# Turning an expert tile's token rows and another tile's gated values together, in 64-row halves of the TensorE array

## The chip, the cores and the metric

The kernel runs on one core of a Trainium2 chip. The metric is the device time of one execution in microseconds (us), taken as the median of several runs. Beside it stands one execution that was profiled; times of single instructions come from that one.

## What is computed

Two transformer layers on x of shape 8 x 512 x 256, all in fp32. The first is an attention with relative positions and a feed-forward block with a token-dependent low-rank part; the second a masked attention and a mixture of experts. Only the last part is changed. Cut to it:

```python
tokens = hidden_states.reshape(-1, 256)              # 4096 tokens
topk_idx, topk_w = route(tokens)                     # 4 of 32 experts for each token
gate_vals = silu(einsum('th,eih->tei', tokens, gate_w))   # gate_w: 32 x 128 x 256
up_vals = einsum('th,eih->tei', tokens, up_w)             # up_w:   32 x 128 x 256
expert_out = einsum('tei,ehi->teh', gate_vals * up_vals, down_w)  # down_w: 32 x 256 x 128
mixed = (take(expert_out, topk_idx) * topk_w[:, :, None]).sum(1)
return mixed + shared_expert(tokens)
```

## The kernel before

Earlier stages leave, for every token and each of its four experts, one row of 264 numbers in a DRAM table `rows`, sorted by expert: 256 values of the token, then the place of its result and its weight. The table is cut into NS = 160 tiles of 128 rows, padded so that a tile belongs to one expert. All experts' weights lie in SBUF as `store`, 768 columns an expert: 256 columns of gate and up for each half k of the 256 inputs (NK = 2), and 256 columns of down.

The last stage goes through the 160 tiles, one per step s of a loop whose order is written by hand (`tc.manual_schedule()`), as a software pipeline over tiles. Names and lines are those of the profile:

- `fetch` (L1414) loads a tile r of 128 x 264, by a DMA on SP's queue, eight tiles ahead (TILES = 8). Eleven buffers (TILES + 3) hold r until its rows are scattered.
- `spread` (L1432, L1434) turns the two 128 x 128 halves of r by two TensorE transposes into a PSUM bank `ptr` and copies 128 x 256 to SBUF as `rT` on DVE. In step s it does tile s + 3.
- `numbers` (L1420) reads eight experts' numbers into TensorE registers, every eighth step, ahead of `expert_hidden`.
- `expert_hidden` (L1440, L1444, L1446) multiplies rT with gate and up into `pge`; each of the two products, 256 columns wide, is two matmul instructions in fp32, so a tile has four. ACT makes silu of the gate half, `acte`, and DVE multiplies by the up half, giving `hide`. In step s it does tile s + 2.
- `turned_hidden` (L1451, L1453) turns hide (one 128 x 128 transpose, PSUM bank `pth`) and copies it to `hidT` on DVE. In step s it does tile s + 1.
- `result` (L1458, L1460, L879) multiplies hidT with down into `poe` (two matmul instructions), ACT scales by the row's weight into y, and POOL issues an indirect DMA that scatters y to the table `results`. In step s it does tile s.
- `gather`, `add`, `put` (L1470, L1482, L1485, L1492): as soon as all tiles that a batch of tokens needs are out, its results are gathered on SP's queue, added on DVE and stored; these pieces are spread over later steps.

So TensorE's order in a step is: two transposes of r for tile s + 3, four product instructions for tile s + 2, one transpose of hide for tile s + 1, two product instructions for tile s. Each of the four PSUM pools (`ps_r`, `ps_t`, `ps_e`, `ps_y`) has two banks[...].

The first attention, elsewhere in the same program, turns its weights e in 64-row halves (`turned`, L412, copied at L415). It matters as the place where such instructions are already in the trace:

```python
for f, bank in enumerate(banks):
    rs, c = slice(64 * f, 64 * f + 64), (j * NT + m) * 64
    nc.tensor.transpose(bank[:, c : c + 64], e[rs, m * P : (m + 1) * P], ident[rs, rs])
```

Around it on TensorE stand transposes of 128 rows ahead (L384), then products of 128 rows by 32 columns of the array (L424), and at times products of the whole array after these (L273).

Of the kernel before, what the change touches and what calls it, by code (L numbers as in the profile page):

```python
# [12 lines left out]
F32 = mybir.dt.float32  # L13
# [5 lines left out]
PSUM = bass.MemoryType.PSUM  # L19
DRAM = bass.MemoryType.DRAM  # L20

P = 128
B, S, H = 8, 512, 256
NT = S // P
NK = H // P
# [16 lines left out]
NS = NTOK * TOPK // P + NE  # L42
TILES = 8
ROW = 264
# [757 lines left out]
def _l1(nc, tc, a, x, out, ident, mhalf, rows, results, filled, inputs, early):  # L802
# [14 lines left out]
    with ExitStack() as ctx:  # L817
        pool = lambda name, bufs, **kw: ctx.enter_context(tc.tile_pool(name=name, bufs=bufs, **kw))
# [14 lines left out]
        for half in range(2):  # L833
            s = slice(half * P, (half + 1) * P)
# [36 lines left out]
        def after(ins, others):  # L871
            info = mybir.DependencyInfo(mybir.DependencyClass.Sync, mybir.DependencyReason.DATA)
            for o in others:
                tc.add_manual_dep(ins.ins, o.ins.name, info, reason="rows of DRAM")
# [32 lines left out]
        q, k, v, xlT = {}, {}, {}, {}  # L907
        prods, sums, sc, softs, values, turned = {}, {}, {}, {}, {}, {}
# [472 lines left out]
        for u in range(U):  # L1381
            t = start[u]
# [21 lines left out]
            experts()  # L1404
        routing.close()
        tp = pool("m_t", 2)
        ps_r = pool("m_psr", 2, space=PSUM)
        ps_t = pool("m_pst", 2, space=PSUM)
        ps_e = pool("m_pse", 2, space=PSUM)
        ps_y = pool("m_psy", 2, space=PSUM)  # L1410

        def fetch(s):
            r = tp.tile([P, ROW], F32, tag="r", name="r", bufs=TILES + 3)
            ins = nc.sync.dma_start(r, rows[s * P : (s + 1) * P, :])  # L1414
            after(ins, scattered["rows"][-16:])
            return r

        def numbers(s):

            _, found = nc.values_load_multi_w_load_instructions(  # L1420
                number[0:1, s : s + 8],
                [mybir.EngineType.PE],
                min_val=0,
                max_val=NE - 1,
                skip_runtime_bounds_check_because="all but the bits of an expert's number are masked out",
            )
            return dict(enumerate(found, s))

        def spread(r):
            pt = ps_r.tile([P, S], F32, tag="psr", name="ptr")  # L1430
            for k in range(NK):
                nc.tensor.transpose(pt[:, k * P : (k + 1) * P], r[:, k * P : (k + 1) * P], ident)  # L1432
            rT = tp.tile([P, H], F32, tag="rT", name="rT", bufs=3)
            nc.vector.tensor_copy(rT, pt[:, :H])  # L1434
            return rT

        def expert_hidden(w, rT):
            pg = ps_e.tile([P, S], F32, tag="pse", name="pge")
            for k in range(NK):
                nc.tensor.matmul(  # L1440
                    pg[:, :H], rT[:, k * P : (k + 1) * P], w[:, k * H : (k + 1) * H], start=k == 0, stop=k == NK - 1
                )
            act = tp.tile([P, P], F32, tag="acte", name="acte", bufs=3)
            nc.scalar.activation(act, pg[:, :P], AF.Silu)  # L1444
            hid = tp.tile([P, P], F32, tag="hide", name="hide", bufs=3)
            nc.vector.tensor_tensor(hid, act, pg[:, P : 2 * P], ALU.mult)  # L1446
            return hid

        def turned_hidden(hid):
            pt = ps_t.tile([P, S], F32, tag="pst", name="pth")  # L1450
            nc.tensor.transpose(pt[:, :P], hid, ident)  # L1451
            hidT = tp.tile([P, P], F32, tag="hidT", name="hidT", bufs=3)
            nc.vector.tensor_copy(hidT, pt[:, :P])  # L1453
            return hidT

        def result(w, r, hid):
            po = ps_y.tile([P, S], F32, tag="psy", name="poe")
            nc.tensor.matmul(po[:, :H], hid, w[:, 2 * H :], start=True, stop=True)  # L1458
            y = tp.tile([P, H], F32, tag="y", name="y", bufs=4)
            nc.scalar.activation(y, po[:, :H], AF.Copy, scale=r[:, H + 1 : H + 2])  # L1460
            scatter("results", results, r[:, H : H + 1].bitcast(U32), y, NTOK * TOPK + NS * P - 1)
# [3 lines left out]
        def gather(u, t, sent):  # L1465

            h, p = divmod(u, 4)
            i = NT * (2 * p + t // 2) + 2 * h + t % 2
            z[u, t] = tp.tile([P, TOPK, H], F32, tag="z", name="z", bufs=5)
            ins = nc.sync.dma_start(  # L1470
                z[u, t].rearrange("p k c -> p (k c)"),
                results[i * P * TOPK : (i + 1) * P * TOPK, :].rearrange("(p k) c -> p (k c)", k=TOPK),
            )
            tc.declare_no_dep(ins.ins, group="results", reason="its results are those sent")
            tc.add_to_no_dep_group("gathers", ins.ins)
            after(ins, sent)

        def add(b, t, part):

            w = z[b, t]  # L1480
            if part == 0:
                nc.vector.tensor_tensor(w[:, :2, :], w[:, :2, :], w[:, 2:, :], ALU.add)  # L1482
            else:
                to = _halves(x, b)[t]
                nc.vector.tensor_tensor(to, to, w[:, part - 1, :], ALU.add)  # L1485

        def put(u, t):

            h, p = divmod(u, 4)
            to = out.rearrange("b (t p) c -> b p t c", p=P)  # L1490
            if isinstance(t, tuple):
                nc.sync.dma_start(to[2 * p + t[0], :, 2 * h : 2 * h + 2, :], two_tiles(u, t[0]))  # L1492
            else:
                nc.sync.dma_start(to[2 * p + t // 2, :, 2 * h + t % 2, :], _halves(x, u)[t])
# [4 lines left out]
        def finish(b, s):  # L1499

            sent = scattered["results"][-16:]
            for t in range(NT):
                beside.setdefault(s + 3 + 3 * t, []).append(partial(gather, b, t, sent))
                for part in range(3):
                    beside.setdefault(s + 8 + 3 * t + part, []).append(partial(add, b, t, part))
            for r in range(2):
                beside.setdefault(s + 22 + r, []).append(partial(put, b, (r,)))

        with tc.manual_schedule():


            tiles, which, rTs, made, hidTs = {}, {}, {}, {}, {}
            weights = lambda s: store[:, bass.ds(which[s], 1), :].rearrange("p e c -> p (e c)")
            for s in range(TILES):
                tiles[s] = fetch(s)
            for s in range(-3, NS):
                if 0 <= s < NS - TILES:
                    tiles[s + TILES] = fetch(s + TILES)
                if s + 3 < NS:
                    rTs[s + 3] = spread(tiles[s + 3])  # L1520
                if 0 <= s + 2 < NS:
                    if (s + 2) % 8 == 0:
                        which.update(numbers(s + 2))
                    made[s + 2] = expert_hidden(weights(s + 2), rTs.pop(s + 2))
                if 0 <= s + 1 < NS:
                    hidTs[s + 1] = turned_hidden(made.pop(s + 1))
                if s < 0:
                    continue
                result(weights(s), tiles.pop(s), hidTs.pop(s))
                for f in beside.pop(s, []):  # L1530
                    f()

                n, more = divmod(s + 2 - NE, S * TOPK // P)
                if 0 < n < B and more == 0:
                    finish(n - 1, s)
            for t in range(NT):
                gather(B - 1, t, scattered["results"][-16:])
            for s in sorted(beside):
                for f in beside[s]:
                    f()  # L1540
            for t in range(NT):
                for part in range(3):
                    add(B - 1, t, part)
                put(B - 1, t)
# [140 lines left out]
```

## Time and profile before

| what | us |
|---|---|
| median of 3 runs | 2083.9 (2081.64 to 2084.47) |
| the profiled execution, whole | 2102.91 |
| its span, first to last instruction | 2101.1 |
| first transpose of the expert tiles starts at | 1816.5 |
| first result product (tile 0) starts at | 1823.9 |
| last result product (tile 159) starts at | 2089.2 |
| TensorE busy in 1834 to 2087 | 249.4 of 253.0 |
| DVE, ACT, POOL busy in the same stretch | 160.6, 112.9, 147.2 |
| granted TensorE clock, 1816 to 1827 and 1827 to 2087 | 0.68 and 1.00 |

In the lines of the profile a matmul instruction's time runs from its start to its modelled end, and instructions overlap in the array; what a stream of them costs is therefore read from one start to the next, not from the sum of times. In a line of the timeline "xN" is a number of instructions on end, the first number where the first of them starts, the second the time from there to the end of the last. "64*128" is the part of the array that an instruction uses, in rows and columns; L1440's and L1458's instructions are "128*128". PEld is the load of the stationary operand, which can run ahead under an earlier matmul.

### The profile page before, as it was taken

The page shows a single profiled execution, that of the slowest core. Times are in us where ns is not written, and L with a number is a line of the kernel's source. Part 1 is how long each engine was busy: PE and PEld are TensorE (multiplying, and loading weights), DVE is VectorE, ACT ScalarE, POOL GpSimd, SP SyncE. Part 2 cuts the span into 40 slices and gives each one's busy share as a digit, 9 for nine tenths or more (in the row PEclk, how much of TensorE's full clock was granted, in tenths as well). Part 3 has the DMA queues.
Part 4 walks back from the last instruction along what each step waited for, and adds up shares of the span by engine and source line. Part 5 has one row for each costly group of instructions (what it writes and reads, how often), then busy time and mean ns, then how long its engine had stood idle before and what let it go on. Part 6 is the DMA issues. An engine that isn't in the chain of part 4 may idle for free.

```text
span 2101.1 us, 49496 instructions
## 1 busy us (share of the span) xinstructions
PE 1930.6 (92%) x17956; PEld 1334.9 (64%) x17956; DVE 1389.0 (66%) x3731; ACT 1106.3 (53%) x2366; POOL 1143.3 (54%) x1340
## 2 busy tenths in 40 slices
PE   7999999999999999999889999879888778599997
PEld 4666667666666666676656666545455455388786
DVE  3677777777777777777676454257876775356666
ACT  2677777767777777677631222345433422144443
POOL 4666777767778686776733111114444443455555
PEclk7999999999999999999989999999989987699999
DMA  8999999999999999899944548601111115457888
GB/s 270 305 317 284 310 303 300 292 289 304 295 297 304 296 306 299 286 289 299 285 140 143 167 141 127 20 1 42 42 42 42 42 42 215 169 163 217 256 254 266
DMA packets 388928, 444.43 MB, mean 212 GB/s; under 512 B 43344, under 2 KB 367952, under 8 KB 388688
## 3 DMA queue, kind: packets, MB, share of 16 engines
q1 hardware_dynamic: 373904, 401.93, 63.9%
q0 software_dynamic: 13824, 38.29, 5.0%
q8 instruction: 145, 2.38, 0.5%
q10 hardware_dynamic: 960, 1.05, 0.1%
q14 instruction: 95, 0.78, 0.1%
HBM read 238.99 MB, written 202.19 MB: 210 GB/s over the span
## 4 chain that ended last, share of the span: by engine, by line
PE 63%; DVE 11%; DMA 11%; issue 5%; POOL 5%; ACT 3%; SPq 1%; another core or an unknown queue 0%; POOLq 0%; DVEq 0%; ACTq 0%
PE sc L372 7%; PE sc L384 6%; PE pge L1440 6%; PE et_ps L412 5%; PE po L684 5%; DMA winp<-shift 5%; PE ctx_ps L424 5%; PE pq L291 5%; PE ph L676 3%; PE poe L1458 3%; PE pa L315 3%; DMA shift<-strip 3%; PE pq L935 2%; PE po L460 2%; DVE prod L796 2%
## 5 line engine op out<-in xcount | busy, mean ns | idle before, releaser
L398 DVE CUSTOM_DVE_ANT_0 e<-sc,winc 128x512 f32<-128x512 f32 x512 | 333.3, 689 | 268.1 <-PE sc L384 139.4
L401 ACT ACTIVATE e<-e,low 128x512 f32<-128x512 f32 x512 | 365.7, 715 | 94.8 <-DVE low L398 93.5
L322 ACT COPY strip<-pa 128x512 f32<-128x512 f32 x512 | 275.2, 591 | 138.6 <-POOL winc L352 58.2
L325 POOL TENSOR_TENSOR own<-aside,strip 128x512 f32<-128x512 f32 x256 | 269.1, 1051 | 130.3 <-ACT strip L322 121.6
L415 DVE COPY et<-et_ps 128x512 f32<-128x512 f32 x512 | 328.5, 683 | 0.7 <-PE et_ps L412 0.7
L372 PE MATMUL sc<-sm,sm 32*128 32x256 f32 (+3 forms) x1792 | 310.5, 437 | 0.2
L315 PE MATMUL pa<-pos,sm 32*128 32x256 f32 x2048 | 297.2, 407 | 1.7 <-ACT sm L299 1.0
L879 POOL DMA_INDIRECT rows<-pay,slot x128 | 141.4, 1105 | 237.2 <-issue 224.9
L352 POOL TENSOR_TENSOR winp<-winp,own 128x256 f32<-128x256 f32 x256 | 187.3, 732 | 108.0 <-DMA winp<-shift 78.3
L372 PEld LDWEIGHTS sc<-sm,sm 32*128 32x128 f32 x1792 | 164.1, 184 | 97.0 <-DVE et L415 35.6
L384 PE MATMUL sc<-ident,winp 128*128 128x128 f32 x1280 | 204.9, 287 | 22.4 <-DMA winp<-shift 21.1
L879 POOL DMA_INDIRECT results<-y,r x160 | 157.0, 981 | 124.3 <-ACT y L1460 70.7
L352 POOL TENSOR_TENSOR winc<-winc,own 128x256 f32<-128x256 f32 x256 | 187.2, 731 | 52.2 <-DMA winc<-shift 40.6
L384 PEld LDWEIGHTS sc<-ident,winp 128*128 128x128 f32 x1280 | 137.4, 142 | 102.0 <-issue 58.3
L315 PEld LDWEIGHTS pa<-pos,sm 32*128 32x128 f32 x2048 | 178.5, 187 | 11.5 <-issue 2.0
L412 PE MATMUL et_ps<-ident,e 64*128 64x64 f32 x4096 | 184.2, 230 | 1.1 <-DVE et L415 1.1
L58 POOL TENSOR_TENSOR rstd<-var,mhalf 128x2 f32<-128x2 f32 (+1 forms) x56 | 51.1, 912 | 241.5 <-DVE var L56 208.9
L412 PEld LDWEIGHTS et_ps<-ident,e 64*128 64x128 f32 x4096 | 148.9, 140 | 44.4 <-issue 22.8
L1440 PE MATMUL pge<-store,rT 128*128 x640 | 168.0, 385 | 3.5 <-DVE rT L1434 1.1
L424 PE MATMUL ctx_ps<-et,v 128*32 128x128 f32 x4096 | 166.6, 281 | 0.5 <-DVE et L415 0.5
L291 PE MATMUL pq<-xnT,wqk 128*128 128x512 f32 x256 | 134.0, 646 | 0.1
L679 ACT ACTIVATE hT<-ph,b 128x512 f32<-128x512 f32 x64 | 44.0, 687 | 165.6 <-PE ph L676 165.5
(216 smaller groups left out, 3339.0 us busy)
## 6 DMA issues: line engine op xcount, KB each, us to landing
shift<-strip SPq DMA_DIRECT2D x256, 510.0 KB
winp<-shift SPq DMA_DIRECT2D x128, 384.0 KB
winc<-shift SPq DMA_DIRECT2D x128, 384.0 KB
winp<-shift SPq DMA_DIRECT2D x128, 256.0 KB
winc<-shift SPq DMA_DIRECT2D x128, 256.0 KB
rows<-empty SPq DMA_DIRECT2D x8, 2640.0 KB
r<-rows SPq DMA_DIRECT2D x160, 132.0 KB
z<-results SPq DMA_DIRECT2D x32, 512.0 KB
```

The costliest lines, as they stand in the source:

```text
L315: nc.tensor.matmul(pa[:, t * W : (t + 1) * W], src[rs, i * P : (i + 1) * P], pos[rs, g, :], start=True, stop=True)
L322: nc.scalar.copy(st[:, 2 * j : 2 * j + 2, :].rearrange("p t w -> p (t w)"), pas[j])
L352: nc.gpsimd.tensor_tensor(dst, dst, own[:, t], ALU.add)
L372: nc.tensor.matmul(sc[:, c0:c1], s[side_][rs, cut : cut + P], s[2 + side_][rs, c0:c1], start=c0 == 0, stop=False, skip_group_check=True,)
L384: nc.tensor.matmul(sc[:, m * P : (m + 1) * P], wins[n + 2 * (m - i)][1][:, j, (i - m + 1) * P : (i - m + 2) * P], ident, start=False, stop ...
L398: nc.vector.tensor_tensor_reduce(e, sc, wins[n][0][:, j, :], 1.0, -LOW, ALU.add, ALU.min, low)
L401: nc.scalar.activation(e, e, AF.Exp, bias=low, scale=-1.0, accum_out=totals[b, g // 2][:, i, r : r + 1])
L412: nc.tensor.transpose(bank[:, c : c + 64], e[rs, m * P : (m + 1) * P], ident[rs, rs])
L415: nc.vector.tensor_copy(et[:, f].rearrange("p j m q -> p (j m q)"), bank)
L424: nc.tensor.matmul(ctx_ps[32 * r : 32 * r + 32, i * P : (i + 1) * P], vs[b % 2][:, m, g % 2, g // 2 * 4 + r, :], et[:, :, m, :], start=m = ...
L879: ins = nc.gpsimd.indirect_dma_start(to, bass.IndirectOffsetOnAxis(ap=index, axis=0), source, None, bounds_check=last)
L1440: nc.tensor.matmul(pg[:, :H], rT[:, k * P : (k + 1) * P], w[:, k * H : (k + 1) * H], start=k == 0, stop=k == NK - 1)
```

## The change

- A new `turned(r, hid)` takes the place of `spread` and `turned_hidden`. In step s it turns r of tile s + 4 and hide of tile s + 1 into one PSUM tile of two banks, each 128 x 128 transpose as two transposes of 64 rows: rows 0 to 63 into the first bank, rows 64 to 127 into the second, the two alternating. One DVE copy moves all 128 x 384 to SBUF.
- `expert_hidden` runs for tile s + 3 in step s, `result` for tile s as before. So hide now lies two steps ahead of where it is turned and not one, and the loop starts at s = -4.
- The PSUM pool `ps_r` goes; `ps_t` holds two tiles of two banks. r has twelve buffers, hide four.
- TensorE's order in a step: six half transposes, four product instructions for tile s + 3, two for tile s. The orders of SP's and POOL's queues stay as they were.

```diff
-            r = tp.tile([P, ROW], F32, tag="r", name="r", bufs=TILES + 3)
+            r = tp.tile([P, ROW], F32, tag="r", name="r", bufs=TILES + 4)
...
-        def spread(r):
-            pt = ps_r.tile([P, S], F32, tag="psr", name="ptr")
-            for k in range(NK):
-                nc.tensor.transpose(pt[:, k * P : (k + 1) * P], r[:, k * P : (k + 1) * P], ident)
-            rT = tp.tile([P, H], F32, tag="rT", name="rT", bufs=3)
-            nc.vector.tensor_copy(rT, pt[:, :H])
-            return rT
+        turns = lambda out, rows: [
+            nc.tensor.transpose(out[:, f, :], rows[64 * f : 64 * f + 64], ident[64 * f : 64 * f + 64, 64 * f : 64 * f + 64])
+            for f in range(2)
+        ]
+
+        def turned(r, hid):
+
+            pt = ps_t.tile([P, 2, S], F32, tag="pst", name="pt")
+            parts = []
+            if r is not None:
+                parts += [(k, r[:, k * P : (k + 1) * P]) for k in range(NK)]
+            if hid is not None:
+                parts.append((NK, hid))
+            for k, rows in parts:
+                turns(pt[:, :, k * 64 : (k + 1) * 64], rows)
+            out = tp.tile([P, NK + 1, 2, 64], F32, tag="turned", name="turned", bufs=3)
+            ks = slice(parts[0][0], parts[-1][0] + 1)
+            nc.vector.tensor_copy(
+                out[:, ks].rearrange("p k f t -> p f k t"),
+                pt[:, :, : (NK + 1) * 64].rearrange("p f (k t) -> p f k t", t=64)[:, :, ks],
+            )
+            return out.rearrange("p k f t -> p (k f t)")
...
-            hid = tp.tile([P, P], F32, tag="hide", name="hide", bufs=3)
+            hid = tp.tile([P, P], F32, tag="hide", name="hide", bufs=4)
...
-        def turned_hidden(hid):
-            pt = ps_t.tile([P, S], F32, tag="pst", name="pth")
-            nc.tensor.transpose(pt[:, :P], hid, ident)
-            hidT = tp.tile([P, P], F32, tag="hidT", name="hidT", bufs=3)
-            nc.vector.tensor_copy(hidT, pt[:, :P])
-            return hidT
...
-            for s in range(-3, NS):
+            for s in range(-4, NS):
...
-                if s + 3 < NS:
-                    rTs[s + 3] = spread(tiles[s + 3])
-                if 0 <= s + 2 < NS:
-                    if (s + 2) % 8 == 0:
-                        which.update(numbers(s + 2))
-                    made[s + 2] = expert_hidden(weights(s + 2), rTs.pop(s + 2))
-                if 0 <= s + 1 < NS:
-                    hidTs[s + 1] = turned_hidden(made.pop(s + 1))
+                if s + 1 < NS:
+                    both = turned(tiles[s + 4] if s + 4 < NS else None, made.pop(s + 1, None))
+                    rTs[s + 4], hidTs[s + 1] = both[:, :H], both[:, H:]
+                if 0 <= s + 3 < NS:
+                    if (s + 3) % 8 == 0:
+                        which.update(numbers(s + 3))
+                    made[s + 3] = expert_hidden(weights(s + 3), rTs.pop(s + 3))
```

More of the change, by code (lines that the diff above doesn't have):

```diff
@@ L1406, in _l1 @@
         tp = pool("m_t", 2)
-        ps_r = pool("m_psr", 2, space=PSUM)
         ps_t = pool("m_pst", 2, space=PSUM)
```

## The prediction, made before the changed kernel had run

> **What bounds the kernel now.** I read the busy times of the page first, then the stretch of the expert tiles alone, then the timeline of TensorE in it. The page says that TensorE is busy for 92% of the span; in the stretch from 1834 to 2087 us it is busy 249.4 of 253.0 us, with the clock at 1.00, while DVE stands at 160.6 and POOL at 147.2. Busy matmul records overlap, so what a tile costs is read from starts:
>
> ```profile
> 1953.61 0.38 PE L1432 MATMUL ptr<-ident,r 128*128 128x128 f32 x2
> 1953.83 1.03 PE L1440 MATMUL pge<-store,rT 128*128 x4
> 1954.70 0.27 PE L1451 MATMUL pth<-ident,hide 128*128 128x128 f32 x1
> 1954.81 0.60 PE L1458 MATMUL poe<-store,hidT 128*128 x2
> 1955.24 0.38 PE L1432 MATMUL ptr<-ident,r 128*128 128x128 f32 x2
> ```
>
> A tile takes 1955.24 - 1953.61 = 1.63 us (1628 ns by the start records), without an idle time in brackets. It is two transposes at 109 ns, four products at 216, one transpose at 109, two products at 217. All are 128*128. So TensorE is the bound here, and whatever changes its instructions moves the end tile by tile. The waits of TensorE in this stretch come to little:
>
> ```profile
> PE pge L1440 <- DVE rT L1434: 1.1, 2, 0.6
> PE poe L1458 <- DVE hidT L1453: 0.9, 1, 0.9
> PE pge L1440 <- ACT y L1460: 0.8, 2, 0.4
> ```
>
> From tile 0's result (1823.88) to tile 159's (2089.24) there are 265.4 us; 159 tiles at 1.628 are 258.8. The 6.6 us left are the only slack that a deeper pipeline can recover. Most of them recur every eighth tile, where the experts' numbers are read into registers (L1420): in the chain of waits, in order of time, such a place reads
>
> ```profile
> 2060.90 0.22 PE ptr L1432 x2
> 2061.12 0.11 issue
> 2061.23 1.10 PE pge L1440 x4
> 2062.33 0.11 PE pth L1451
> ```
>
> 0.3 us late and with four products in 1.10 us, where 1.03 in the timeline above is usual.
>
> **What the changed order will contain.** Half transposes occur already, in the first attention. The timeline of TensorE there:
>
> ```profile
> 803.24 0.87 PE L384 MATMUL sc<-ident,winp 128*128 128x128 f32 x6
> 804.05 0.71 PE L412 MATMUL et_ps<-ident,e 64*128 64x64 f32 x16
> 804.69 0.64 PE L424 MATMUL ctx_ps<-et,v 128*32 128x128 f32 x16
> ...
> 800.53 0.65 PE L424 MATMUL ctx_ps<-et,v 128*32 128x128 f32 x16
> 801.10 1.13 PE L273 MATMUL pv<-wv,xnT 128*128 128x256 f32 x4
> ```
>
> A last start is the end of the group less one instruction's own time: 273 ns for L384 and L424, 223 for L412, 379 for L273 (medians of their lines). Read that way:
> - The last L384 starts at 803.84, the first half at 804.05: 0.20 us (203 ns, the shortest and the median of the 255 such places), where two 128-wide transposes on end stand 109 apart. So 94 ns are lost.
> - Sixteen halves take 0.71 - 0.22 = 0.49 us from first to last start, in pairs: the second pair starts 112 ns after the first, later ones about 63 apart. Six halves: 112 + 63 + 3 = 178 ns.
> - From the last half (804.54) to L424: 150 ns, where 54 to 64 would follow. About 90 are lost again.
> - L273 after L424: 202 ns, not 109, so again 93; and its four products need 1.13 - 0.38 = 0.75 us from first to last start, where L1440 needs 1.03 - 0.38 = 0.65. The first load of weights was not hidden: 104 ns.
>
> [...]
> - [...]every change of the array's form costs 90 to 96 ns beyond the streaming, in both directions.
> - [...]the halves of a pair start 3 to 4 ns apart and a pair takes 63 ns against 109.
> - [...]The first product after a change of form is late by 104[...].
>
> **The change, part by part.**
>
> *Transposes.* Removed: three at 109, 326 ns a tile. Added: six halves between whole-array products, thus two changes of form in every tile. Sum of a tile by the durations above: last product of a tile to the first half 216 + 93 = 309; six halves 178; last half to the first product 150; first to second product 216 + 104 = 320; then the four remaining steps 216, 216, 216, 218 = 866. Together 1823 ns against 1628: 195 ns longer. The three pairs alone, at 63, would have saved 137; the two changes of form with their cold loads cost 332. For 160 tiles: +31.2 us. No instruction stands between 64*128 and 128*128 directly in the trace; I take L424's form for the first and L424 to L273 for the last, as every pair of forms that occurs costs about the same. Bounds: as low as 290 ns for both (the first half's load partly hidden by other work) gives 24.5 us; 350 gives 34.
>
> *Ends of the loop.* Two or three more changes of form in steps without a full set: +0.9 us.
>
> *A step deeper.* hide is made two steps before it is turned. TensorE's queue reaches the read of the numbers earlier, since the load that waited for hide finds it ready; a late read is also covered in part by the cold load that is paid anyway. Of 6.6 us I take 5.5 as gained, a choice, since one place (0.9 us, behind hidT) is of another kind; bounds 0 and 6.6.
>
> *DVE.* Two copies, 418 (128x256) and 283 (128x128), become one. L415's 128x512 takes 682, so a column block of 128 costs about 135 and 128x384 about 550; 150 less a tile. This counts for nothing: DVE is busy 160.6 of 253.0 us. The cover is the 1.8 us of a step; with hide (288) and the largest add (681) DVE needs 1.52 us. If it went over, TensorE would wait by the difference.
>
> *New wait.* The first half transpose waits for r of tile s + 4, hide of tile s + 1 and its two banks, and behind it stand the products of both other tiles, for which ACT, then POOL's scatter wait. hide now comes from products a whole step (1.8 us) further back, and is rarely waited for even today (0.2 us in all by PEld's waits). r is fetched at the same step and used four steps later instead of five: 7.3 us against 8.1; its buffer comes free a tile earlier in exchange (twelve). The tile view has TensorE waiting for r once, at the start, 23.1 us. SP's and POOL's orders stay, and each gets more time per tile. Cost: nothing, bound +5 us if r is late under the gathers.
>
> *Sum.* 31.2 + 0.9 - 5.5 = +26.6 us. The profiled execution of 2102.9 us (span 2101.1) would become 2129.5. The runs' median is 19 us below that execution; this stage is bound by TensorE at full clock, so I carry the difference over: 2083.9 + 26.6 = 2110.5, rounded to 2110.
>
> **Rivals.**
> 1. *Whole gain[...]* (ends faster). If the queue loaded the halves' weights under the products before[...], a tile is 137 ns shorter: -21.9, and -5.5 from the numbers: 2056 us. It decides once both changes cost under 137 + 34 = 171 ns a tile. For it: halves do pair at 63 ns. Against it: the same 203 ns at 255 places, and three other pairs of forms with 93.
> 2. [...]93 + 96 paid, 104 and 49 not. A tile is 43 ns longer: +6.9 + 0.5 - 5.5, so 2086. Against it: 0.75 for L273's four.
> 3. *Worse*: the stalls stay, or r or the copy is late, or the halves run one after another because the banks clash (six at 55 or more, 0.15 us a tile): +38 to +50, 2122 to 2134. Against it: L412's pairs go to two banks in the same way.
> That the order is not as written I exclude: built, TensorE's list shows four halves of r, two of hide, the products, step for step.
>
> **How the numbers follow.** The forecast (2102 to 2119 by its own bounds) has 0.82, the whole gain 0.05, the second rival 0.06, the worse case 0.07. About 0.2% is what a measurement of this kernel can tell from no change, that is 2079.7 to 2088.1: faster 0.05, within 0.05, slower 0.90. The range goes from 2099 (cheap changes and the whole slack) to 2122.
>
> **What would show it.** In the changed trace: a tile period near 1.82 us; about 309 ns from the last result product to the first half; 150 from the last half to a product; four products in about 1.13 us instead of 1.03; one copy of about 550 ns; hardly a gap every eighth tile. A period under 1.63 makes me wrong, and then the gap before the first half, or the first load after the halves, must be shorter than in the first attention. A period above 1.9 with idle TensorE would name r or the copy.

## The result and the profile after

The changed kernel takes 2109.3 us (median of 4 runs, 2106.08 to 2112.87) against 2082.8 (4 runs, 2079.99 to 2084.47): a ratio of 1.0123, 95% interval 1.0100 to 1.0147, or 26.5 us more, where 26.6 were forecast. Its profiled execution, 2110.6 us with a span of 2108.8, lies among its runs. The one of before, 2102.9, lay 19 above its own: there, everything ahead of the expert tiles took 15.6 us longer (first transpose at 1816.5 us, in the changed kernel at 1800.9), which is no part of the change. So spans of these two profiles must not be subtracted; stages can be compared.

The timeline of TensorE in the changed kernel, one tile and the start of the next:

```profile
1954.20 0.34 PE L1430 MATMUL pt<-ident,r 64*128 64x64 f32 x4
1954.38 0.23 PE L1430 MATMUL pt<-ident,hide 64*128 64x64 f32 x2
1954.53 1.13 PE L1455 MATMUL pge<-store,turned 128*128 x4
1955.50 0.59 PE L1466 MATMUL poe<-store,turned 128*128 x2
1956.03 0.34 PE L1430 MATMUL pt<-ident,r 64*128 64x64 f32 x4
```

A tile takes 1956.03 - 1954.20 = 1.83 us, where it took 1.63. The start records of all tiles give the parts (medians): last result product to first half 310 ns (forecast 309), first to last of the six halves 177 (178), last half to first product 152 (150), first product to second 320 (320). The four products take 1.13 us from first start to last end, not 1.03.

Where the time goes shows in the loads of the stationary operand (PEld). Before, a load starts while the instruction ahead of it still runs, 0.11 us ahead of the first gate and up product (1953.83) and 0.21 ahead of the first transpose (1955.24):

```profile
1953.72 0.73 PEld L1440 LDWEIGHTS pge<-store,rT 128*128 128x128 f32 x4
1955.03 0.36 PEld L1432 LDWEIGHTS ptr<-ident,r 128*128 128x128 f32 x2
```

In the changed kernel the loads at the same two places start no earlier than their matmuls:

```profile
2079.01 0.73 PEld L1455 LDWEIGHTS pge<-store,turned 128*128 128x128 f32 x4
2079.01 1.13 PE L1455 MATMUL pge<-store,turned 128*128 x4
2080.50 0.20 PEld L1430 LDWEIGHTS pt<-ident,r 64*128 64x128 f32 x4 [0.33 <-PE pge L1455]
2080.50 0.34 PE L1430 MATMUL pt<-ident,r 64*128 64x64 f32 x4
```

The waits of PEld (total us, times, longest) in the changed kernel, from 1834 to 2100 us:

```profile
PEld pt L1430 <- PE pge L1455: 44.4, 134, 0.3
PEld pt L1430 <- issue: 3.6, 11, 0.3
PEld pge L1455 <- ACT y L1468: 1.0, 2, 0.6
```

At nearly every tile the first half's load stands idle for 0.33 us (44.4 us at 134 places). The releaser named, "pge", ended some 0.4 us earlier (2079.01 + 1.13, against 2080.50), and from the last result product to the first half pass 310 ns at all 158 places recorded, shortest and longest included, where 217 passed to the first transpose before. The two waits for ACT's y in the lines above, 0.6 us and 0.4, differ from each other. So I take it that no data is waited for. That the load starts late by a fixed time is read from the trace; what it waits for there is not shown. The groups of the same stretch:

```profile
L1446 DVE COPY turned<-pt 128x384 f32<-128x384 f32 x142 | 78.7, 554 | 11.8 <-PE pt L1430 11.8
L1466 PE MATMUL poe<-store,turned 128*128 x292 | 87.0, 380 | 0.1
L1430 PE MATMUL pt<-ident,r 64*128 64x64 f32 x568 | 47.9, 247 | 0.0
```

The joint copy takes 554 ns (forecast about 550), and TensorE's own matmuls wait for nearly nothing.

### The profile page after: what moved, and what is told of

Its sections match the earlier page's. It is cut to its first block, busy times and chain, and to the rows that moved or that the text cites. A ratio compares the mean times of both kernels' runs of the same rounds, so it can differ in the third digit from the quotient of the medians.

```text
span 2108.8 us, 50144 instructions
## 1 busy us (share of the span) xinstructions
PE 1952.4 (93%) x18436; PEld 1323.3 (63%) x18436; DVE 1381.3 (66%) x3574; ACT 1106.1 (52%) x2366; POOL 1140.7 (54%) x1340
## 4 chain that ended last, share of the span: by engine, by line
PE 56%; DMA 12%; DVE 11%; POOL 9%; issue 7%; ACT 4%; SPq 1%; another core or an unknown queue 0%; POOLq 0%; DVEq 0%; ACTq 0%
PE sc L372 6%; PE sc L384 5%; PE po L684 5%; PE pge L1455 5%; PE et_ps L412 5%; DMA winp<-shift 5%; PE ctx_ps L424 4%; PE pq L291 4%; DMA shift<-strip 3%; PE ph L676 2%; PE pa L315 2%; POOL results L879 2%; PE poe L1466 2%; DMA winc<-shift 2%; ACT strip L322 2%
## 5 line engine op out<-in xcount | busy, mean ns | idle before, releaser
L384 PE MATMUL sc<-ident,winp 128*128 128x128 f32 x1280 | 202.9, 286 | 18.6 <-DMA winp<-shift 17.5
L384 PEld LDWEIGHTS sc<-ident,winp 128*128 128x128 f32 x1280 | 137.1, 141 | 96.7 <-issue 55.9
L315 PEld LDWEIGHTS pa<-pos,sm 32*128 32x128 f32 x2048 | 178.5, 187 | 11.5 <-issue 2.0
L412 PE MATMUL et_ps<-ident,e 64*128 64x64 f32 x4096 | 183.7, 229 | 1.1 <-DVE et L415 1.1
L1455 PE MATMUL pge<-store,turned 128*128 x640 | 182.7, 408 | 1.7 <-DMA r<-rows 0.9
L412 PEld LDWEIGHTS et_ps<-ident,e 64*128 64x128 f32 x4096 | 148.4, 139 | 44.0 <-issue 21.8
L1459 ACT ACTIVATE acte<-pge 128x128 f32<-128x128 f32 x160 | 44.3, 277 | 186.0 <-PE pge L1455 139.3
L291 PE MATMUL pq<-xnT,wqk 128*128 128x512 f32 x256 | 133.0, 642 | 0.1
```

The lines of the kernel that those rows point to most:

```text
L315: nc.tensor.matmul(pa[:, t * W : (t + 1) * W], src[rs, i * P : (i + 1) * P], pos[rs, g, :], start=True, stop=True)
L384: nc.tensor.matmul(sc[:, m * P : (m + 1) * P], wins[n + 2 * (m - i)][1][:, j, (i - m + 1) * P : (i - m + 2) * P], ident, start=False, stop ...
L1455: nc.tensor.matmul(pg[:, :H], rT[:, k * P : (k + 1) * P], w[:, k * H : (k + 1) * H], start=k == 0, stop=k == NK - 1)
```

## The experiments

**Theory.** Going from the whole array to 64-row halves and back costs 332 ns each time (some 95 beyond the usual spacing at each of the two changes, by the first attention's starts, and the rest, by my estimate, first loads that start no earlier than their matmuls), and the halves save 137 ns of transposing a tile; the rest of the change removes gaps at the reads of the experts' numbers. **Rivals.** The price lies in each half transpose; or in the joint copy or the new order; or the deeper pipeline does nothing by itself.

In the table a kernel's stage is cut at TensorE's starts: from the first transpose to the first gate and up product (fill), to the last tile's first one (steady part), to the last result product (run-out), to the end of the span (tail). The beat is the time of one tile: the median over all stretches of eight tiles between tiles 20 and 148, divided by eight. All are in us.

| kernel, one profile each | fill | steady | run-out | tail | beat |
|---|---|---|---|---|---|
| before, first profile | 1.6 | 268.2 | 3.1 | 11.7 | 1.658 |
| before, again | 1.7 | 266.1 | 3.6 | 12.0 | 1.644 |
| changed | 1.6 | 291.3 | 3.5 | 11.5 | 1.823 |
| whole transposes, deeper | 1.7 | 260.0 | 5.3 | 11.4 | 1.625 |
| groups of two, halves | 2.3 | 264.0 | 4.5 | 12.6 | 1.653 |
| groups of four, halves | 4.7 | 254.3 | 10.0 | 10.6 | 1.575 |
| groups of four, whole | 5.0 | 257.2 | 9.6 | 10.6 | 1.623 |
| groups of four, halves, numbers read early | 4.2 | 251.6 | 9.3 | 10.8 | 1.568 |

Ratios below are to the kernel before, run beside them on the same chip: 2076.1 us beside the halves undone, the four changes and the groups with halves, 2076.4 beside the whole groups, the shallow version and the one row group, 2078.1 beside the early numbers. A difference in us is the ratio's, with the ends of its 95% interval in brackets.

### The halves undone

```diff
             for k, rows in parts:
-                turns(pt[:, :, k * 64 : (k + 1) * 64], rows)
+                nc.tensor.transpose(pt[:, k * P : (k + 1) * P], rows, ident)
```

> The changed kernel with the 64-row halves undone: each transpose is one of 128 rows into one bank, the joint copy and the deeper pipeline stay. Theory (the halves cost by their two changes of form, the depth gains): beat 1.628 us a tile, few gaps at the reads of the numbers, so before minus some 8 us: about 2075 us. Rival (the depth gains nothing by itself, the gaps only hid under the cold loads of the halves): beat 1.628 with the gaps of before, 2081 to 2084. Rival (the halves are not what costs, but the joint copy or the order): about 2105.

Measured: 2073.6 us, ratio 0.9984 (0.9969 to 0.9998), 3.3 us less (0.4 to 6.4). TensorE's timeline:

```profile
1953.26 0.38 PE L1443 MATMUL pt<-ident,r 128*128 128x128 f32 x2
1953.48 0.27 PE L1443 MATMUL pt<-ident,hide 128*128 128x128 f32 x1
1953.59 1.03 PE L1452 MATMUL pge<-store,turned 128*128 x4
1954.45 0.59 PE L1463 MATMUL poe<-store,turned 128*128 x2
1954.88 0.38 PE L1443 MATMUL pt<-ident,r 128*128 128x128 f32 x2
```

The beat is 1.62 us again, with a joint copy of the same size (554 ns), the order and the depth of the changed kernel. So these three cost nothing, and the halves carry the whole loss. The gaps (starts later than is usual for their pair of instructions) sum to 3.6 us in the stage, 10.7 and 8.6 in the two profiles of before. The steady part lost 6 to 8 us, of which 1.7 to 2.2 came back in the run-out, so the stage is 4.4 to 5.8 us shorter. The gain in the runs, 3.3 us, is less than half of the 8 forecast.

### Four changes of form a tile

The order and depth of before, each transpose split where it stands; both kinds of transpose now share the two tiles of `ps_t`:

```diff
-            pt = ps_r.tile([P, S], F32, tag="psr", name="ptr")
+            pt = ps_t.tile([P, 2, S], F32, tag="pst", name="ptr")
             for k in range(NK):
-                nc.tensor.transpose(pt[:, k * P : (k + 1) * P], r[:, k * P : (k + 1) * P], ident)
+                turns(pt[:, :, k * 64 : (k + 1) * 64], r[:, k * P : (k + 1) * P])
...
-            nc.tensor.transpose(pt[:, :P], hid, ident)
+            turns(pt[:, :, :64], hid)
```

> The kernel before, its order and depth kept, with each of its transposes as two halves in place: the rows of tile s + 3, products, the gated values of tile s + 1, products. There are four changes of form a tile and the same six halves as in the changed kernel. Theory (price by changes): beat 1.628 - 0.137 + 2 x 0.332 = 2.155 us, +84 us, 2160 to 2167 us. Rival (price by halves): beat 1.82, 2110 to 2115.

Measured: 2152.0 us, ratio 1.036 (1.0329 to 1.0391), 75 us more (68 to 81). TensorE's timeline:

```profile
1954.04 0.34 PE L1429 MATMUL ptr<-ident,r 64*128 64x64 f32 x4
1954.31 1.13 PE L1446 MATMUL pge<-store,rT 128*128 x4
1955.37 0.28 PE L1429 MATMUL pth<-ident,hide 64*128 64x64 f32 x2
1955.57 0.70 PE L1464 MATMUL poe<-store,hidT 128*128 x2
1956.20 0.34 PE L1429 MATMUL ptr<-ident,r 64*128 64x64 f32 x4
```

The tile is 2.16 us (theory 2.155, the price-by-halves rival 1.82), with the same six halves. Both kinds of product are now stretched behind the halves, 1.13 for 1.03 and 0.70 for 0.60. The rival falls. From a product to the first half behind it pass 310 ns here too (medians, at both places of a tile), so the shared PSUM tiles add nothing there. That the runs show 75 and not 84 has its cause in the trace: the gaps are down to 1.7 us, from 9 to 11, though nothing is deeper here. The reads of the numbers start 1.57 us ahead of their products here, 1.14 in the kernel before.

### The same halves, gathered in groups

`turned` takes two or four tiles' rows and gated values on end, and the pipeline is deeper by what that needs: for four, rows are fetched 17 tiles ahead and products made for tile s + 6, for two 11 ahead and tile s + 4. The code of the groups of four:

```diff
-                if s + 1 < NS:
-                    both = turned(tiles[s + 4] if s + 4 < NS else None, made.pop(s + 1, None))
+                if (s + 10) % GROUP == 0 and s + 1 < NS:
+                    both = turned(
+                        {j: tiles[s + 10 + j] for j in range(GROUP) if s + 10 + j < NS},
+                        {j: made.pop(s + 1 + j) for j in range(GROUP) if 0 <= s + 1 + j < NS},
+                    )
```

> As the groups of four, with two tiles on end. Theory: beat 1.628 - 0.137 + 0.332/2 = 1.657 us, 4.6 us more than before, 8 less from the gaps: about 2079 us. Rival (price in each half): about 2107.

> Halves as in the changed kernel, but four tiles' rows and four tiles' gated values are turned on end, then four tiles' products follow; the pipeline is deeper by what that needs (products for tile s + 6, rows up to s + 13, fetch 17 ahead). Theory (332 ns for each way into the halves and back, 137 ns saved a tile by pairs): beat 1.628 - 0.137 + 0.332/4 = 1.574 us on the average, 8.6 us less than before in all, some 8 more from the gaps, 1 to 3 back in a longer tail: 2066 to 2070 us. Rival (the price is in each half transpose, not in the change of form): beat 1.82, about 2107. Rival (at 1.57 another engine or the fetch ends last): gaps of TensorE, 2075 to 2090.

> The groups of four with whole 128-row transposes, no change of form: tells what the grouping costs by itself. Theory (pairs save 137 ns a tile, a change of form and back costs 332 a group): 1.628 a tile plus the same gaps at the reads of the numbers as in the groups of four with halves, so 8 to 9 us slower than those: +7 to +10 us against before. Rival (the halves gain nothing even in groups): same as the groups with halves.

Measured: groups of two 2080.1 us, ratio 1.0021 (1.0007 to 1.0035); groups of four 2074.8, ratio 1.0002 (0.9986 to 1.0017); groups of four with whole transposes 2078.0, ratio 1.0007 (0.9994 to 1.0020). The beats are those of the theory: 1.653 (1.657), 1.575 (1.574), 1.623 (1.628). A group of four in TensorE's timeline:

```profile
1955.69 0.34 PE L1431 MATMUL pt<-ident,r 64*128 64x64 f32 x4
1955.87 0.23 PE L1431 MATMUL pt<-ident,hide 64*128 64x64 f32 x2
...
1956.58 1.13 PE L1465 MATMUL pge<-store,turned 128*128 x4
1957.55 0.59 PE L1476 MATMUL poe<-store,turned 128*128 x2
1957.98 1.03 PE L1465 MATMUL pge<-store,turned 128*128 x4
1958.85 0.59 PE L1476 MATMUL poe<-store,turned 128*128 x2
```

Only the first product group behind the halves takes 1.13; the next is back at 1.03. So the beat does gain by halves once enough of them stand together. The times, though, missed the expectations by 14 us (four halves) and 8 (two), and the whole groups of four, expected 7 to 10 us above before, are 1.5 above (-1.2 to 4.2). In time, then, halves and whole transposes in these groups of four cannot be told apart (1.0002 and 1.0007). Only part of the misses shows in the table. With groups of four and halves the steady part is 12 to 14 us shorter than before, and the fill takes 3.0 and the run-out 6.6 more. The run-out of the groups of four:

```profile
2053.94 1.96 PE L1476 MATMUL poe<-store,turned 128*128 x6
2057.65 0.70 PE L1476 MATMUL poe<-store,turned 128*128 x2 [1.75 <-ACT y L1478]
2058.28 0.27 PE L1431 MATMUL pt<-ident,hide 64*128 64x64 f32 x2
2058.48 1.22 PE L1476 MATMUL poe<-store,turned 128*128 x2
2061.55 1.22 PE L1476 MATMUL poe<-store,turned 128*128 x2 [1.85 <-ACT y L1478]
```

Six tiles' results are still to be made when the last gate and up products are done, and then TensorE waits for ACT's y, which itself waits for the scatters that POOL issues (ACT stands idle for 2.0 us until 2057.12, ended by one of these transfers). Whole transposes in the same groups lose as much at both ends (5.0 and 9.6), so this belongs to the depth, not to the halves.

The profiles give the groups of two a stage of 270.8 us, 1.4 us under the mean of before's two (272.9 and 271.5), and the runs 4.4 us more than before, with a tail of 12.6. One profile a kernel does not settle such a difference; where it comes from stays open.

### The numbers read early

```diff
                 if 0 <= s + 6 < NS:
-                    if (s + 6) % 8 == 0:
-                        which.update(numbers(s + 6))
                     made[s + 6] = expert_hidden(weights(s + 6), rTs.pop(s + 6))
+                if (s + 8) % 8 == 0 and s + 8 < NS:
+                    which.update(numbers(s + 8))
```

> The groups of four with halves, with the read of the experts' numbers moved behind the third tile's products of the group ahead of the one that needs it, away from the place straight behind the 24 halves. Theory (of the 8.6 us that fewer changes of form save, some 3.5 were given back at these reads, the rest in a longer fill and tail): stage 265 to 266 us instead of 269.0, 3 to 4 us under the groups of four, 0.15 to 0.2% under before. Rival (the reads only show a wait that moves elsewhere): stage 268 to 270, same time as the groups of four.

Measured: 2072.8 us, ratio 0.9982 (0.9968 to 0.9996), 3.7 us less than before and 0.2% less than the groups of four by their ratios; the stage is 265.0 us (expected 265 to 266, groups of four 269.0). In the groups of four the register read starts 0.8 us ahead of its product and takes 0.59 to 1.28. TensorE's timeline there shows one of the longer waits that follow, in brackets; eight of them sum to 2.9 us, and after the first tile the reads together delay their products by some 4.0:

```profile
1949.68 0.23 PE L1431 MATMUL pt<-ident,hide 64*128 64x64 f32 x2
1950.32 1.13 PE L1465 MATMUL pge<-store,turned 128*128 x4 [0.41 <-issue]
```

With the reads out of the way the halves' gain shows beyond the beat: against the whole groups of four, whose products wait little at their own reads, the stage is 6.7 us shorter (265.0 and 271.8), and the ratios to before are 0.9982 and 1.0007, some 5 us apart, though in different sets and with intervals that just touch.

This and the whole transposes with the deeper pipeline are the two versions under the kernel before, both by about 0.2% and barely clear of no change; their intervals do not tell them apart.

### No step deeper

Whole transposes and the joint copy, the depth of before:

```diff
-                    both = turned(tiles[s + 4] if s + 4 < NS else None, made.pop(s + 1, None))
-                    rTs[s + 4], hidTs[s + 1] = both[:, :H], both[:, H:]
-                if 0 <= s + 3 < NS:
+                    both = turned(tiles[s + 3] if s + 3 < NS else None, made.pop(s + 1, None))
+                    rTs[s + 3], hidTs[s + 1] = both[:, :H], both[:, H:]
+                if 0 <= s + 2 < NS:
```

> Whole 128-row transposes and the joint copy, but without the step deeper: products for tile s + 2 and rows of s + 3 in step s, so the gated values are turned right after the step in which their products ran. Theory (the joint turn needs the depth): between those products' end and the turn stands only one result product pair (0.43 us), while ACT, DVE and their hand-overs need some 0.9 to 1.0, so TensorE waits about 0.5 us a tile: beat 2.1 to 2.2, +75 to +95 us against before. Rival (depth is not needed): within 5 us of before.

Measured: 2138.9 us, ratio 1.0299 (1.0264 to 1.0333), 62 us more. The timeline of all engines, cut to the path:

```profile
1952.24 0.59 PE L1463 MATMUL poe<-store,turned 128*128 x2
1952.44 0.28 ACT L1456 ACTIVATE acte<-pge 128x128 f32<-128x128 f32 x1 [1.01 <-PE pge L1452]
...
1952.75 0.29 DVE L1458 TENSOR_TENSOR hide<-acte,pge 128x128 f32<-128x128 f32 x1 [0.56 <-ACT acte L1456]
...
1953.10 0.33 PE L1443 MATMUL pt<-ident,hide 128*128 128x128 f32 x1
```

From product to silu, gate and turn takes 0.66 us from ACT's start; the turn comes some 0.2 us late. Its load stands idle for 0.28 us until hide is there and starts at 1953.09, with the turn; in the kernel before it started 0.22 us ahead of it (1954.48 and 1954.70). Tiles are 1.92 us apart, and the reads of the numbers add 0.7 to 1.1 every eighth tile, a beat of 2.03. The 62 us are fewer than the 75 to 95 expected: I had put the wait at 0.5 us a tile; it is 0.3, and the reads add 0.1. In this loop a joint turn needs the depth.

### Both halves on one row group

Rows 64 to 127 of every tile are left out; rows 0 to 63 are turned twice:

```diff
-            nc.tensor.transpose(out[:, f, :], rows[64 * f : 64 * f + 64], ident[64 * f : 64 * f + 64, 64 * f : 64 * f + 64])
+            nc.tensor.transpose(out[:, f, :], rows[:64], ident[:64, :64])
```

> The changed kernel, but both half transposes of a pair read rows 0 to 63 (the rows 64 to 127 of every tile are left out of the computation), so that both use the same row group of the array; the number of instructions, changes of form, banks and copies is the same. Theory (pairs share the time of one because they lie on different row groups): the six halves take about 330 ns from first to last start instead of 178, beat 1.97, some 24 us above the changed kernel. Rival (a half costs its issue, whatever the row group): beat 1.82, same time as the changed kernel.

Measured: 2134.6 us, ratio 1.0277 (1.0247 to 1.0308), 58 us more than before, some 31 more than the changed kernel's 26.5 (24 were expected; the stage is 28 us longer, 324.7 and 296.5). TensorE's timeline:

```profile
1955.06 0.46 PE L1430 MATMUL pt<-ident,r 64*128 64x64 f32 x4
1955.36 0.28 PE L1430 MATMUL pt<-ident,hide 64*128 64x64 f32 x2
1955.57 1.13 PE L1455 MATMUL pge<-store,turned 128*128 x4
1956.54 0.59 PE L1466 MATMUL poe<-store,turned 128*128 x2
1957.06 0.46 PE L1430 MATMUL pt<-ident,r 64*128 64x64 f32 x4
```

From the first half to the product 0.51 us pass, in the changed kernel 0.33; everything else is as there. On one row group a half takes 62 ns, as long as a pair on two; the expectation had 54. So pairing works in the changed kernel (six halves in 177 ns), and the rival that halves run one after another there falls.

### Before, once more

> The kernel before, unchanged, profiled once more: how far the expert stage differs between executions. In the first profile it took 272.9 us from the first transpose to the last result product, 10.7 of them gaps. Theory (the changed kernel's runs lie 26.5 us above, its stage only 23.5, because that profile caught large gaps at the reads of the numbers): 269 to 271 us here. Rival (the rest lies elsewhere): 272 to 274.

Measured, in one run: a stage of 271.5 us, first transpose to last result product, with 8.6 us of gaps (first profile: 272.9 and 10.7), and 2076.1 us in all. It falls between the two expectations. The first transpose starts at 1790.9 us here, 25.6 us earlier than in the first profile, which confirms that the stages ahead of the change differ so much between executions.

## Why the prediction was right, and where its terms were off

- *TensorE bounds the stage, tile by tile*: right. TensorE is busy for 252.2 of the 253.0 us from 1834 to 2087.
- *The price of changing the form*: right within 2 ns, term by term. Shown by one tile's parts, by the undone halves (1.625), four changes (2.165) and the groups (1.653, 1.575). The prediction says that neither form follows the other directly in the trace. That is wrong: L384 is 128*128 and L412 64*128, so its 203 ns are the way in itself, at 255 places. The way out stands there once, at 63.06 us, where L291 (128*128, 512 columns) follows L412: 152 ns to the first product and 533 to the second, where 430 is usual, so 103 are lost.
- *One load that nothing hides*: in the trace, the first load behind the halves starts with its product (2079.01 for both), where it started 0.11 us ahead before, and the second product starts 320 ns after the first, where 216 is usual: 104 late. That the load makes these 104 ns is an inference: records of such loads last 190 ns (L1440), and no run isolates it.
- *+31.2 us for 160 tiles*: 160 x (1823 - 1628) holds; the steady part alone grew by 23 to 25 us, since it also lost gaps.
- *The gaps, 5.5 us*: too small. Gaps fell from 10.7 (8.6 in the other profile) to 2.8, so 6 to 8 went. I had put the slack at 6.6 by 159 whole tiles from first to last result; but the last two steps make no gate and up products (2 x 0.87 us), so the slack was over 8.
- *What removes them*: only half right. I gave it to the depth. The depth does it alone (whole transposes, 3.6 us left), but so do the four changes without depth (1.7 left). A slow beat by itself does not: the shallow version has 2.03 us a tile, and its reads, 1.04 us ahead, still cost 0.7 to 1.1 each. What goes with small gaps is a read that starts early, 1.54 us ahead of its product in the whole transposes, 1.57 with four changes and 1.83 in the changed kernel, where it was 1.14; what lets it start early in each is not isolated.
- *DVE, the new wait, r's shorter lead*: nothing, as forecast. The joint copy is 554 ns; r is waited for at the start alone.
- *The ends, +0.9 us*: fill and run-out together differ from before by -0.2 to +0.4 us.
- *The sum*: the stage grew by 23.5 us against the first profile and 25.0 against the second, the runs by 26.5 (20.8 to 30.6 by the interval). The forecast of 26.6 is inside; that it meets the median so closely is luck, since the stage itself grew by 1.5 to 3 us less, and that part of the runs' difference has no cause shown.

Of the rivals, the one of the whole gain and the one without cold loads fell by the changed kernel's timeline (310 ns and 1.13 us); the worse one by the row-group run and by the waits.

## What to carry to other kernels

In this kernel, using the array in halves for a few small transposes pays by how many of them stand together, not by how many there are: here 137 ns saved a tile against 332 for each way in and back, so a single tile loses, a group of two still loses a little (a beat of 1.653 us against 1.625), a group of four gains (1.575 against 1.623 for the same groups whole). Read the price of such a change from another place in the same trace where the two forms meet, from start to start (203 ns into the halves there, 150 out), and include what the products behind it are late by (104 more at L273). Gains in the beat of a deep pipeline can be given back at its ends: in the groups of four the steady part is 12 to 14 us shorter and the fill 3.0 and the run-out 6.6 longer, with TensorE waiting up to 1.85 us for ACT's y behind the scatters.

## What was not expected of the hardware

- A 64-row fp32 transpose takes 62 ns from start to start on one row group, and a pair on two row groups takes 63. So a half alone does not take half of the 109 of a whole one, which would be 54.
- Reading eight registers takes TensorE's queue from 0.59 us (groups of four) to 1.88 (changed kernel), and how far ahead of its product it starts differs with the order: 1.14 us before, 1.83 in the changed kernel, 0.8 behind 24 halves, 2.2 behind twelve whole transposes (groups of four, whole).
- Scatters on POOL last 0.97 us, but on end they start 1.27 us apart at the least in the profiles of before and of the changed kernel. POOL in the groups of four with the early reads, at the end:

```profile
2049.05 0.97 POOL L880 DMA_INDIRECT results<-y,r  x1 [0.30 <-ACT y L1478]
2050.33 0.97 POOL L880 DMA_INDIRECT results<-y,r  x1 [0.30 <-ACT y L1478]
2051.61 0.97 POOL L880 DMA_INDIRECT results<-y,r  x1 [0.30 <-issue]
```

Six of them take some 7.7 us by this spacing (an estimate, 6 x 1.28), most of the run-out of 9.3 to 10.0 us in the groups of four.
